# Filling a selective-scan pipeline: finer turns for TensorE and ScalarE, later sums from two banks

## The chip, the cores and the metric

One core of one Trainium2 chip. The metric is the device time of one launch in microseconds; lower is better.

## The reference

The input is four images of 64 x 64 positions with 128 channels, so 4 x 4096 tokens. The whole network is a Mamba-like layer, an attention layer and an expert layer with a residual sum after each. Only the first is touched by the change:

```python
x = x + _L0_conv_ref(_gn(x), ...)           # _gn: group norm, 32 groups

xz = einsum('pd,bld->bpl', in_proj_w, x)     # 256 channels x, 256 channels z
def mamba_dir(xz, ...):
    x, z = split(xz, 2)
    x = silu(causal_conv1d(x, conv_w, conv_b))           # 4 taps
    x_dbl = einsum('rd,bdl->brl', x_proj_w, x)           # 8 dt, 16 B, 16 C rows
    delta = softplus(einsum('dr,brl->bdl', dt_w, dt_raw) + dt_b)
    A = -exp(A_log)
    h = h * exp(delta * A) + (delta * x) * B             # scan over 4096 positions
    y = sum over 16 states of h * C
    return (y + D * x) * silu(z)
y = y_forward + y_backward + y_sliced        # three orders of the same tokens
out = einsum('od,bdl->blo', out_proj_w, y)
```

All is float32.

## The kernel before

The launch has four stretches. In the **fill**, the class Inputs makes what the scans of all four images need and writes it to DRAM, while the class Scans already runs the scans of image 0 beside it. In the **wide opening** the first attention input is made from image 0's sums. In the **main loop** attention of one image runs beside the scans of the next. An end part follows. The change lies in the fill and in the few lines around it.

**Inputs** handles an image in a norm (`norm`, L254 on), and then twelve chunks (three orders of four chunks with 1024 positions each, `of_chunk`). In a chunk, PE makes the convolution into two PSUM tiles `cv` (the input projection is folded into its taps), ACT makes `u` by Silu, PE makes the projection `xd` (copied by ACT to `xds`) and from it `dt`. The softplus is max(v, 0) + log(1 + exp(-|v|)), with a correction for the rounding of 1 + e: ACT makes `e` by Abs and then Exp, `r` by Relu, `ln` by Ln, and `s` in two Identity steps; PE adds e, -s and ln in PSUM (`sp`, L415), and DVE adds this to r (L417) and multiplies it with u (L421). Chunks of order 2 are each followed by a `gate`, which makes silu(z). These pieces are Python generators. `flow` (L79) keeps up to two of them active and takes one turn of each alternately; every yield ends a turn. A second piece may start when the youngest active one has had `apart` turns, in which turns that yield WAIT don't count, but plain waiting yields do. The PSUM tiles of Inputs are three tiles of two banks each that rotate; `held` counts those in use. `middle` lets only one chunk at a time be between dt and the last r.

**Scans** (`of_image`) runs 384 steps for an image: 3 orders x 4 chunks x 8 groups of channels x 4. A step handles 128 rows (16 channels x 8 states) of 1024 positions: ACT makes `dA` = exp(A delta) (L496, written in place into `delta` in odd steps), DVE multiplies `dB` = du x B (L505), scans to `h` (L508) and multiplies with C in place (L510). For each four steps PE sums over the states into a PSUM tile `y` (L516): the sums of steps 0 and 1 are issued at turn 1 of the next four steps, those of 2 and 3 at turn 2, and at the end of that turn DVE makes the output `o` (L532) and the bank goes back. `delta` has three buffers of two steps each, `du` four, `dB` three, dA two. For image 0 the loads of `du` are issued by ACT, all others by SP (L482).

Everything in the fill is issued in an order written out by hand, and each engine works its own queue in that order. Two `Pace` objects set it: per iteration 0.98 turns of the flow and one turn of the scans, a step of the scans being two turns:

```python
first = Pace(scans.of_image(0, inputs.made, nc.scalar))
others = Pace(flow(inputs.pieces(range(nb)), 2, 6))
while not first.done:
    others.run(0.98)
    first.run(1.0)
others.rest()
```

Of the kernel before, what the change touches and what calls it, by code (L numbers as in the profile page):

```python
# [81 lines left out]
WAIT = "wait"  # L82
# [52 lines left out]
def scan_weights(nc, const, load, load_ps, ident, in_proj_w, out_proj_w, dirs):  # L135

    w_z = const["fill"].tile([P, DI], F32, name="w_z")
    w_out = const["all"].tile([P, 2, C], F32, name="w_out")
    w_in = load.tile([P, 4, C], F32, tag="w_in", name="raw_in")
    nc.sync.dma_start(out=w_in, in_=in_proj_w.rearrange("(k p) c -> p k c", p=P))  # L140
    ps = load_ps.tile([P, 512], F32, tag="ps", name="ps_in")
    for m in range(2):
        nc.tensor.transpose(ps[:, m * P : (m + 1) * P], w_in[:, 2 + m, :], ident)
    nc.vector.tensor_copy(w_z, ps[:, :DI])
    raw = load.tile([P, DI], F32, tag="raw", name="raw_out")
    nc.sync.dma_start(out=raw, in_=out_proj_w)
    ps = load_ps.tile([P, 512], F32, tag="ps", name="ps_out")
    for m in range(2):
        nc.tensor.transpose(ps[:, m * P : (m + 1) * P], raw[:, m * P : (m + 1) * P], ident)
    nc.vector.tensor_copy(w_out.rearrange("p m c -> p (m c)"), ps[:, :DI])  # L150
    ws = []
    for i, d in enumerate(dirs):
        w = {}
        raw = load.tile([R + 2 * NS, DI], F32, tag="raw", name=f"raw_x{i}")
        nc.sync.dma_start(out=raw, in_=d["x_proj_w"])
        w["x"] = const["fill"].tile([P, 2, X_ROWS], F32, name=f"w_x{i}")
        nc.gpsimd.memset(w["x"], 0.0)
        for m in range(2):
            ps = load_ps.tile([P, 512], F32, tag="ps", name=f"ps_x{i}_{m}")
            k = R + 2 * NS  # L160
            nc.tensor.transpose(ps[:, :k], raw[:, m * P : (m + 1) * P], ident[:k, :k])
            for row, at, n in ((DT_ROW, 0, R), (B_ROW, R, NS), (C_ROW, R + NS, NS)):
                nc.vector.tensor_copy(w["x"][:, m, row : row + n], ps[:, at : at + n])
        raw = load.tile([P, 2, X_ROWS], F32, tag="raw_dt", name=f"raw_dt{i}")
        nc.gpsimd.memset(raw, 0.0)
        nc.sync.dma_start(out=raw[:, :, DT_ROW:], in_=d["dt_proj_w"].rearrange("(m p) r -> p m r", p=P))
        w["dt"] = const["fill"].tile([X_ROWS, 2, P], F32, name=f"w_dt{i}")
        ps = load_ps.tile([P, 512], F32, tag="ps", name=f"ps_dt{i}")
        for m in range(2):
            nc.tensor.transpose(ps[:X_ROWS, m * P : (m + 1) * P], raw[:, m, :], ident)  # L170
        nc.vector.tensor_copy(w["dt"][DT_ROW:].rearrange("r m p -> r (m p)"), ps[DT_ROW:X_ROWS, :DI])
        for name in ("conv_b", "dt_proj_b"):
            w[name] = const["fill"].tile([P, 2], F32, name=f"{name}{i}")
            nc.scalar.dma_start(out=w[name], in_=d[name].rearrange("(m p) -> p m", p=P))

        w["D"] = const["all"].tile([P, DI // 32], F32, name=f"D{i}")
        for g in range(4):
            nc.scalar.dma_start(out=w["D"][32 * g : 32 * g + 32], in_=d["D"].rearrange("(k p) -> p k", p=32))

        taps = load.tile([P, 2, 4], F32, tag="taps", name=f"taps{i}")  # L180
        nc.scalar.dma_start(out=taps, in_=d["conv_w"].rearrange("(m p) k -> p m k", p=P))
        w["conv"] = const["fill"].tile([P, 4, DI], F32, name=f"conv{i}")
        for k in range(4):
            ps = load_ps.tile([P, 512], F32, tag="ps", name=f"ps_cv{i}_{k}")
            for m in range(2):
                cut = load.tile([P, C], F32, tag="cut", name=f"cut{i}_{k}_{m}")
                nc.vector.tensor_scalar_mul(cut, w_in[:, m, :], taps[:, m, k : k + 1])
                nc.tensor.transpose(ps[:, m * P : (m + 1) * P], cut, ident)
            nc.vector.tensor_copy(w["conv"][:, k, :], ps[:, :DI])
        ws.append(w)  # L190
    for i, (d, w) in enumerate(zip(dirs, ws)):

        w["A"] = const["all"].tile([P, 2, NB // 2], F32, name=f"A{i}")
        a_log = d["A_log"].rearrange("(k d) (q n) -> d q n k", d=16, n=NS2)
        for c in range(16):
            for q, by in enumerate((nc.scalar, nc.gpsimd)):
                by.dma_start(out=w["A"][c * NS2 : (c + 1) * NS2, q, :], in_=a_log[c, q])
        nc.scalar.activation(w["A"], w["A"], AF.Exp)
        nc.vector.tensor_scalar_mul(w["A"], w["A"], -1.0)
    return w_z, w_out, ws  # L200


class Inputs:
# [28 lines left out]

    def bank(self, name):
        while self.held == 3:
            yield
        self.held += 1
        return self.ps.tile([P, T], F32, tag="a", name=name)

# [16 lines left out]
    def norm(self, b):  # L255

        nc = self.nc
        while b - 1 in self.gated and self.gated[b - 1] < NC:
            yield
        self.gated[b] = 0  # L260
        xin = self.x[b].rearrange("(t p) c -> p t c", p=P)
        xn = self.big.tile([P, L + 6], F32, tag="xn", name=f"xn_{b}")
# [51 lines left out]
    def gate(self, b, g):  # L314
        nc, xn = self.nc, self.normed[b]
        s_g = self.piece.tile([P, 2, T], F32, tag="u", bufs=2, name=f"z_{b}_{g}")
        for m in range(2):
            ps = yield from self.bank(f"z_{b}_{g}_{m}")
            for i in range(T // 512):
# [3 lines left out]
                    start=True, stop=True,  # L323
                )
            yield
            nc.scalar.activation(s_g[:, m, :], ps, AF.Silu)
            self.leave()
        nc.gpsimd.dma_start(out=self.sz[b].rearrange("(m p) t -> p m t", p=P)[:, :, g * T : (g + 1) * T], in_=s_g)
# [2 lines left out]

    def of_chunk(self, b, order, c):
        while b not in self.normed or (order == 2 and b not in self.sliced):
            yield
        src = self.sliced[b] if order == 2 else self.normed[b]
        nc, w, key = self.nc, self.ws[order], f"{b}_{order}_{c}"
        made = {
# [20 lines left out]
        for m in range(2):  # L358
            ps = yield from self.bank(f"cv_{key}_{m}")
            for g, cut in enumerate(halves):  # L360
                for k in range(4):
                    nc.tensor.matmul(  # L362
                        ps[:, cut], w["conv"][:, k, m * P : (m + 1) * P], reads(k, g), start=(k == 0), stop=(k == 3)
                    )
            banks.append(ps)
            yield
        for m in range(2):
            nc.scalar.activation(u[:, m, :], banks[m], AF.Silu, bias=w["conv_b"][:, m : m + 1])
            self.leave()
# [12 lines left out]
        yield  # L382

        while self.middle:
            yield
        self.middle = True

        e = self.piece.tile([P, 2, T], F32, tag="e", name=f"e_{key}")
# [14 lines left out]
        s = self.piece.tile([P, 2, T], F32, tag="s", name=f"s_{key}")  # L403
        ln = self.piece.tile([P, 2, T], F32, tag="ln", name=f"ln_{key}")
        nc.scalar.activation(e, e, AF.Exp, scale=-1.0)
        nc.scalar.activation(ln, e, AF.Ln, bias=1.0)
        yield
        nc.scalar.activation(s, e, AF.Identity, bias=1.0)
        nc.scalar.activation(s, s, AF.Identity, bias=self.minus_one)  # L409
        yield  # L410
        for m in range(2):
            ps = yield from self.bank(f"sp_{key}_{m}")
            for cut in halves:
                for i, (sign, t) in enumerate(((self.ident, e), (self.minus, s), (self.ident, ln))):
                    nc.tensor.matmul(ps[:, cut], sign, t[:, m, cut], start=(i == 0), stop=(i == 2))  # L415
            yield
            nc.vector.tensor_add(r[:, m, :], r[:, m, :], ps)  # L417
            self.leave()
        self.middle = False
        keep("delta", r)  # L420
# [6 lines left out]
class Scans:  # L427
# [20 lines left out]
            )  # L448
        self.sums, self.steps, self.did = {}, {}, set()

    def of_image(self, b, made, queue=None):

        nc = self.nc
        self.steps[b] = 0
# [15 lines left out]
        def load(s):  # L470
# [7 lines left out]
            for name, bufs in (("delta", 3), ("du", 4)):  # L478
                t = self.deep.tile([P, T], F32, tag=name, bufs=bufs, name=f"{name}_{b}_{s}")
                src = made[b, order, c][name][at : at + 16]  # L480
                by = queue if queue is not None and name == "du" else nc.sync
                by.dma_start(out=t, in_=src.unsqueeze(1).to_broadcast([16, NS2, T]))  # L482
                tiles[name, s] = tiles[name, s + 1] = t
            if j == 0:
# [71 lines left out]
        for s in range(self.AHEAD):  # L556
            yield from have(s)
            load(s)
        exp(0)
        y = None  # L560

        def sums(s):

            if s % 4 in (1, 2):
                first = s // 4 * 4 - 4 + (0 if s % 4 == 1 else 2)
                total(first, y)
                total(first + 1, y)

        for s in range(n):
            if s + self.AHEAD < n:  # L570
                yield from have(s + self.AHEAD)
            late = s >= 4 and s % 4 in (1, 2)
            if late and s % 4 == 1:
                while not self.bank.free:
                    self.did.add("wait")
                    yield
# [3 lines left out]
            if s + 1 < n:  # L580
                exp(s + 1)
                self.did.add("exp")
            if late:
                sums(s)
                self.did.add("sum")
            yield
            step(s)
            if late and s % 4 == 2:
                out(s - 3, y)
                self.bank.leave()  # L590
            yield
            self.steps[b] += 1
        while not self.bank.free:
            self.did.add("wait")
            yield
        y = self.bank.grab(f"y_{b}_{n}")
        for s in (n + 1, n + 2):
            sums(s)
            yield
        out(n - 1, y)  # L600
        self.bank.leave()
        self.steps[b] += 1


# [684 lines left out]
def tile_kernel(tc, ctx, x, in_proj_w, dirs, out_proj_w, attn, gate, weight1, weight2, out):  # L1289
# [8 lines left out]
    ident = const.tile([P, P], F32, name="ident")  # L1298
    make_identity(nc, ident)
    cols = column(nc, const, 1e-5, "eps"), column(nc, const, -0.5, "mhalf")  # L1300
    bank = Bank(ctx.enter_context(tc.tile_pool(name="bank", bufs=1, space=PSUM)), 1)
    all_const = ctx.enter_context(tc.tile_pool(name="w_all", bufs=1))
    ws = []
    scanning = ExitStack()
    scans = Scans(tc, scanning, ws, ident, bank, dram)
    with ExitStack() as fill:
        consts = {"all": all_const, "fill": fill.enter_context(tc.tile_pool(name="w_fill", bufs=1))}
        with tc.tile_pool(name="w_load", bufs=2) as load, tc.tile_pool(
# [2 lines left out]
            w_z, w_out, made = scan_weights(nc, consts, load, load_ps, ident, in_proj_w, out_proj_w, dirs)  # L1311
        ws.extend(made)
        inputs = Inputs(tc, fill, x, w_z, ws, cols, dram, ident)
        with tc.manual_schedule():
            first = Pace(scans.of_image(0, inputs.made, nc.scalar))
            others = Pace(flow(inputs.pieces(range(nb)), 2, 6))
            while not first.done:
                others.run(0.98)
                first.run(1.0)
            others.rest()  # L1320
    block = Attention(tc, ctx, attn, gate, cols, ident, bank, dram, t1, w_out, scans.sums, inputs.sz, x)

    following = Pace(*(scans.of_image(b, inputs.made) for b in range(1, nb)))
# [93 lines left out]
```

## Time and profile before

| | |
|---|---|
| median of 3 runs | 13271.63 us (13271.44 to 13279.25) |
| the profiled execution | 13276.74 us, of which span 13275.0 us |
| PE, DVE, ACT, POOL busy, share of the span | 93%, 68%, 81%, 26% |
| first scan of image 0 | at 148.94 us |
| last output of image 0's scans | at 2463.47 us |
| first activation of the main loop | at 2705.9 us |
| TensorE clock granted, whole span and fill | 0.947 and 0.86 |

The shares are means over stretches that differ. The fill, from 147.6 to 2463.9 us, is 17% of the span and the only stretch that the change touches beside the start. Lines "engine ... <- releaser" give idle time of an engine by what ended it: microseconds in total, times, longest.

### The profile page before, as it was taken

The numbers are of one execution on the slowest core, as the hardware profiler recorded it, in microseconds if no ns is written. First come the engines' busy times: TensorE is split into PE (matmuls) and PEld (weight loads), VectorE is DVE, ScalarE is ACT, GpSimd is POOL, SyncE is SP. The second block draws the span as 40 slices with busy tenths as digits, with TensorE's granted clock in tenths as the row PEclk, the third lists the DMA queues.
The fourth block names the chain that finished last, engine by engine and source line by source line (L and its number), as shares of the span: only waits on it lengthen the run. The fifth ranks groups of instructions, "written<-read, shape, count | busy, mean of one in ns | idle before, by whom it ended". The sixth has DMA issues, their size and how long they took to land. (4 is left out here: it accounts for less than half of the span.)

```text
span 13275.0 us, 213812 instructions
## 1 busy us (share of the span) xinstructions
PE 12311.7 (93%) x85255; PEld 3959.8 (30%) x85255; DVE 8963.1 (68%) x8565; ACT 10702.1 (81%) x10807; POOL 3471.0 (26%) x4198
## 2 busy tenths in 40 slices
PE   7797879489999999999999999999999999999976
PEld 3333333222222222233332222333222222222224
DVE  6998989788888876988888778888874110000014
ACT  5665756289999998999999989999998888888851
POOL 2333334222333332333333223333331000000001
PEclk9888888699999999999999999999999999999986
DMA  5666666544444445544444454444443100000015
GB/s 143 185 185 176 190 175 195 172 127 118 121 121 117 115 119 136 130 109 117 114 106 114 116 140 126 110 114 114 112 107 96 43 16 9 9 18 21 12 36 180
DMA packets 686881, 1482.04 MB, mean 112 GB/s; under 512 B 184894, under 2 KB 301942, under 8 KB 685878
## 3 DMA queue, kind: packets, MB, share of 16 engines
q1 hardware_dynamic: 495182, 1049.44, 30.7%
q0 software_dynamic: 139584, 300.84, 7.3%
q10 hardware_dynamic: 51112, 118.08, 3.3%
q8 instruction: 667, 10.93, 0.3%
q14 instruction: 336, 2.75, 0.1%
HBM read 1158.83 MB, written 308.94 MB: 111 GB/s over the span
## 5 line engine op out<-in xcount | busy, mean ns | idle before, releaser
L851 ACT ACTIVATE e<-s 128x1024 f32<-128x1024 f32 x8192 | 7904.5, 1027 | 1015.6 <-PE s L846 788.9
L846 PE MATMUL s<-qm,qT 32*128 32x512 f32 x32768 | 5416.4, 642 | 109.4 <-DMA qT<-d_q 58.8
L860 PE MATMUL acc<-e,v 128*32 128x512 f32 x32768 | 4387.0, 607 | 23.0 <-ACT av L869 20.0
L509 POOL COPY ends<-h 128x1 f32<-128x1 f32 x1536 | 1835.7, 1195 | 4934.0 <-DVE h L508 4920.3
L846 PEld LDWEIGHTS s<-qm,qT 32*128 32x128 f32 x32768 | 1789.8, 184 | 3266.4 <-issue 1453.6
L860 PEld LDWEIGHTS acc<-e,v 128*32 128x32 f32 x32768 | 647.6, 108 | 3158.2 <-issue 3019.3
L508 DVE TENSOR_TENSOR_SCAN h<-dA,ends,dB 128x1024 f32<-128x1024 f32 x576 | 1374.4, 2386 | 186.1 <-ACT dA L496 128.0
L508 DVE TENSOR_TENSOR_SCAN h<-delta,ends,du 128x1024 f32<-128x1024 f32 x576 | 1354.1, 2351 | 160.0 <-ACT delta L496 88.5
L505 DVE TENSOR_TENSOR dB<-du,B 128x1024 f32<-128x1024 f32 x768 | 935.3, 1218 | 204.3 <-PE y L516 185.8
L496 ACT ACTIVATE dA<-delta,A 128x1024 f32<-128x1024 f32 x768 | 887.9, 1156 | 213.5 <-DMA delta<-d_delta 152.2
L496 ACT ACTIVATE delta<-delta,A 128x1024 f32<-128x1024 f32 x768 | 887.3, 1155 | 180.7 <-PE y L516 170.2
L510 DVE TENSOR_TENSOR du<-h,C 128x1024 f32<-128x1024 f32 x768 | 940.7, 1225 | 26.3
L510 DVE TENSOR_TENSOR dB<-h,C 128x1024 f32<-128x1024 f32 x768 | 940.7, 1225 | 26.3
L505 DVE TENSOR_TENSOR du<-du,B 128x1024 f32<-128x1024 f32 x768 | 933.9, 1216 | 0.0
L875 POOL DMA_DIRECT2D d_ctx<-av x512 | 262.6, 521 | 1646.4 <-ACT av L869 1642.8
L362 PE MATMUL cv<-xn,conv 128*128 128x512 f32 x1024 | 492.2, 640 | 40.6 <-DVE xn L299 26.5
L516 PE MATMUL y<-dB,sel 128*32 128x256 f32 x6144 | 496.0, 396 | 16.4 <-DVE o L532 16.4
L516 PE MATMUL y<-du,sel 128*32 128x256 f32 x6144 | 492.0, 393 | 6.1 <-DVE du L510 6.1
L508 DVE TENSOR_TENSOR_SCAN h<-dA,dB 128x1024 f32<-128x1024 f32 x192 | 446.9, 2328 | 56.8 <-ACT dA L496 35.4
L532 DVE SCALAR_TENSOR_TENSOR o<-us,D,y 128x256 f32<-128x256 f32 x384 | 206.2, 537 | 412.1 <-PE y L516 398.6
L508 DVE TENSOR_TENSOR_SCAN h<-delta,du 128x1024 f32<-128x1024 f32 x192 | 440.1, 2292 | 38.9 <-ACT delta L496 15.3
L415 PE MATMUL sp<-s,minus 128*128 128x512 f32 x384 | 223.1, 665 | 208.2 <-ACT s L409 208.2
(248 smaller groups left out, 7714.6 us busy)
## 6 DMA issues: line engine op xcount, KB each, us to landing
delta<-d_delta SPq DMA_DIRECT2D x768, 512.0 KB
du<-d_du SPq DMA_DIRECT2D x576, 512.0 KB
du<-d_du ACTq DMA_DIRECT2D x192, 512.0 KB
d_u<-u POOLq DMA_DIRECT2D x48, 1024.0 KB, 5.7
B<-d_bc SPq DMA_DIRECT2D x96, 512.0 KB
C<-d_bc SPq DMA_DIRECT2D x96, 512.0 KB
d_delta<-r POOLq DMA_DIRECT2D x48, 1024.0 KB, 5.4
d_du<-u POOLq DMA_DIRECT2D x48, 1024.0 KB, 6.7
```

The costliest lines, as they stand in the source:

```text
L362: nc.tensor.matmul(ps[:, cut], w["conv"][:, k, m * P : (m + 1) * P], reads(k, g), start=(k == 0), stop=(k == 3))
L415: nc.tensor.matmul(ps[:, cut], sign, t[:, m, cut], start=(i == 0), stop=(i == 2))
L496: nc.scalar.activation(tiles["delta", s], t, AF.Exp, scale=A)
L505: nc.vector.tensor_mul(dB, du, spread[order, c, "B", j % 2])
L508: nc.vector.tensor_tensor_scan(h, dA, dB, first, ALU.mult, ALU.add)
L509: nc.gpsimd.tensor_copy(ends[order, c][:, at : at + 1], h[:, T - 1 :])
L510: nc.vector.tensor_mul(dB, h, spread[order, c, "C", j % 2])
L516: nc.tensor.matmul(y[32 * g : 32 * g + 32, : T // 4], self.sel[:, j // 2, :], hC[:, 256 * g : 256 * g + 256], start=(j == 0), stop=(j == 3),)
L846: nc.tensor.matmul(s_ps[:, k, :], qT[at : at + 32, kc * P : (kc + 1) * P], queries[j, qb][at : at + 32, :], start=True, stop=True,)
L851: nc.scalar.activation(e, s_ps, AF.Exp, scale=1.0 / math.sqrt(D))
L860: nc.tensor.matmul(accs[j, qb][32 * k : 32 * k + 32, :], v[:, kc, h * VW : h * VW + 32], es[i][k // 2][:, k % 2, :], start=(kc == 0), stop ...
L875: nc.gpsimd.dma_start(out=self.context[b][h * D : h * D + D, cut], in_=av[32 * k : 32 * k + D, :])
```

## The change

Five edits, all for the fill:

- Turns become smaller: a convolution and an sp group yield after each half of a tile (512 positions), with one more yield before ACT or DVE reads the tiles. Ln comes after s in a turn of its own. r is added for both halves of the channels after both sp groups. The gate has one more yield in each half.
- Yields that only wait become WAIT, which doesn't count for `apart`.
- `apart` goes from 6 to 10 and the pace from 0.98 to 1.5 turns per iteration.
- For image 0 (`alone`), the output o is made at turn 0 of the four steps after those in which the sums were issued, two steps later than before, with two banks for the sums. The fill gets a pool of its own for them; the single `bank` for later stretches is made after the fill.
- A's Exp and its negation move from `scan_weights` to the point in `of_image` just ahead of the first dA.

```diff
-        nc.scalar.activation(w["A"], w["A"], AF.Exp)
-        nc.vector.tensor_scalar_mul(w["A"], w["A"], -1.0)
     return w_z, w_out, ws
...
     def bank(self, name):
         while self.held == 3:
-            yield
+            yield WAIT
...
@@ gate
             yield
+            yield
             nc.scalar.activation(s_g[:, m, :], ps, AF.Silu)
@@ of_chunk
                     nc.tensor.matmul(
                         ps[:, cut], w["conv"][:, k, m * P : (m + 1) * P], reads(k, g), start=(k == 0), stop=(k == 3)
                     )
+                yield
             banks.append(ps)
-            yield
+        yield
         for m in range(2):
             nc.scalar.activation(u[:, m, :], banks[m], AF.Silu, bias=w["conv_b"][:, m : m + 1])
...
         nc.scalar.activation(e, e, AF.Exp, scale=-1.0)
-        nc.scalar.activation(ln, e, AF.Ln, bias=1.0)
         yield
         nc.scalar.activation(s, e, AF.Identity, bias=1.0)
         nc.scalar.activation(s, s, AF.Identity, bias=self.minus_one)
         yield
+        nc.scalar.activation(ln, e, AF.Ln, bias=1.0)
+        yield
+        banks = []
         for m in range(2):
             ps = yield from self.bank(f"sp_{key}_{m}")
             for cut in halves:
                 for i, (sign, t) in enumerate(((self.ident, e), (self.minus, s), (self.ident, ln))):
                     nc.tensor.matmul(ps[:, cut], sign, t[:, m, cut], start=(i == 0), stop=(i == 2))
-            yield
-            nc.vector.tensor_add(r[:, m, :], r[:, m, :], ps)
+                yield
+            banks.append(ps)
+        yield
+        for m in range(2):
+            nc.vector.tensor_add(r[:, m, :], r[:, m, :], banks[m])
             self.leave()
@@ of_image
+        if b == 0:
+            for w in self.ws:
+                nc.scalar.activation(w["A"], w["A"], AF.Exp)
+                nc.vector.tensor_scalar_mul(w["A"], w["A"], -1.0)
         exp(0)
...
+        def finish(s, y):
+            out(s, y)
+            self.bank.leave()
...
-            late = s >= 4 and s % 4 in (1, 2)
-            if late and s % 4 == 1:
+            turn = s % 4 if s >= 4 else None
+            if turn == 1:
...
             step(s)
-            if late and s % 4 == 2:
-                out(s - 3, y)
-                self.bank.leave()
+            if turn == 2 and not alone:
+                finish(s - 3, y)
+            if turn == 0 and alone and s >= 8:
+                finish(s - 5, y)
             yield
             self.steps[b] += 1
+        if alone:
+            finish(n - 5, y)
@@ tile_kernel
-    bank = Bank(ctx.enter_context(tc.tile_pool(name="bank", bufs=1, space=PSUM)), 1)
...
+        scans.bank = Bank(fill.enter_context(tc.tile_pool(name="s_bank", bufs=2, space=PSUM)), 2)
         with tc.manual_schedule():
-            first = Pace(scans.of_image(0, inputs.made, nc.scalar))
-            others = Pace(flow(inputs.pieces(range(nb)), 2, 6))
+            first = Pace(scans.of_image(0, inputs.made, True))
+            others = Pace(flow(inputs.pieces(range(nb)), 2, 10))
             while not first.done:
-                others.run(0.98)
+                others.run(1.5)
                 first.run(1.0)
             others.rest()
+    bank = scans.bank = Bank(ctx.enter_context(tc.tile_pool(name="bank", bufs=1, space=PSUM)), 1)
```

## The prediction

> **What bounds the kernel now.** I read the busy time of the engines by stretches, then the waits of VectorE (DVE) in the scan stretch, then the timelines of the places where it stands still. The stretches: start, fill with the scans of image 0, wide opening, main loop.
>
> ```profile
> 0.00:147.60 147.60, 89.23 (x212) 40.90 (x212) 29.08 (x90) 31.26 (x28) 37.26 (x75) 0.90 0.34 79
> 147.60:2463.90 2316.30, 1921.87 (x6641) 774.27 (x6641) 2118.35 (x1457) 1480.85 (x1190) 810.35 (x942) 0.86 0.64 184
> 2463.90:2705.90 242.00, 39.31 (x200) 30.90 (x202) 162.81 (x327) 22.90 (x18) 45.96 (x59) 0.54 0.57 161
> 2705.90:12813.00 10107.10, 9993.55 (x76612) 2941.63 (x76610) 6444.02 (x6164) 9115.55 (x9493) 2508.55 (x3004) 0.99 0.36 92
> ...
> 1360.00:1560.00 200.00, 196.30 (x638) 79.81 (x637) 193.57 (x131) 146.44 (x116) 77.58 (x97) 0.93 0.68 201
> ```
>
> The third and following numbers are PE, PEld, DVE, ACT, POOL busy. The change touches only the first two stretches, and what follows needs image 0's sums, so time saved before 2463.9 shifts all the rest. In the last line, a good stretch, DVE is busy 96.8%, which is as full as it gets (the rest is gaps of some 0.1 us between instructions). Over the whole fill it is 91.5%. So DVE sets the pace; the waits say what is missing:
>
> ```profile
> DVE o L532 <- PE y L516: 57.9, 22, 5.1
> DVE r L417 <- PE sp L415: 31.9, 14, 6.6
> DVE h L508 <- ACT dA L496: 22.3, 8, 3.9
> DVE dB L505 <- DMA du<-d_du: 18.3, 1, 18.3
> DVE h L508 <- ACT delta L496: 12.9, 12, 3.9
> DVE dB L505 <- PE y L516: 8.0, 3, 2.8
> ```
>
> Without the 18.3, which is the first load ahead of scan 0, and with four small rows that add 3, DVE waits **136 us** in the fill. That is all that the change can win there: 2316 - 136 = 2180, and 2118/2180 is 97%, the fullness of the good stretch. The waits sit in a few places. At an image's beginning (672 to 745) there are five:
>
> ```profile
> 688.88 0.48 DVE L532 SCALAR_TENSOR_TENSOR o<-us,D,y 128x256 f32<-128x256 f32 x1 [4.87 <-PE y L516]
> ...
> 706.82 1.23 DVE L505 TENSOR_TENSOR dB<-du,B 128x1024 f32<-128x1024 f32 x1 [2.82 <-PE y L516]
> 709.78 2.35 DVE L508 TENSOR_TENSOR_SCAN h<-dA,ends,dB 128x1024 f32<-128x1024 f32 x1 [1.73 <-ACT dA L496]
> ...
> 717.61 0.48 DVE L532 SCALAR_TENSOR_TENSOR o<-us,D,y 128x256 f32<-128x256 f32 x1 [4.22 <-PE y L516]
> ```
>
> and on TensorE (PE) their cause:
>
> ```profile
> 672.26 15.55 PE L362 MATMUL cv<-xn,conv 128*128 128x512 f32 x32 [8.13 <-DVE xn L299]
> ...
> 688.74 14.01 PE L362 MATMUL cv<-xn,conv 128*128 128x512 f32 x32
> ```
>
> Two chunks' convolutions go back to back, because the second chunk's waiting turns count towards its distance (6), so both start in lockstep. The same happens at the start: 29.37 us of convolution for two chunks before one projection.
>
> **What the Trainium skill says.** "TensorE: Matmul & The Clock Gate", part 1, says that an idle PE falls to half clock after about 3.4 us and takes about as long to warm up. The trace agrees: after an 8.38 us wait a pair of sp matmuls took 2.07 us, warm 1.02. The same page (architectural detail) calls ACT and DVE strict FIFOs; the trace agrees: a u that waited 13.76 us for cv held the dA behind it. "ScalarE: Activation LUTs", "What ACT_TABLE_LOAD costs", gives 1.28 us plus a drain of 1.38; here loads take 1.283 and no drain shows (u's load ran at 692.62 right after an ACTIVATE that ended at 692.61), so I use 1.28. "PSUM — Partial Sum Buffer" (specifications) gives 8 banks of 2 KiB: three double tiles and two sum banks just fit; no trace of before shows all 8 in use.
>
> **The change part by part.** An iteration is one turn of the scan, half a scan step, about 2.44 us of DVE. I wrote the turns of both versions out from the code, as an order without times; durations below are the rows' (cv half 3.44, xd or dt 3.44, sp half 2.58, y 1.0, Exp or Ln 1.91, s 1.9 and 2.0, dA 1.15 us).
>
> 1. *Pace and groups.* A chunk has 12 turns before at 0.98 per iteration (12.2 iterations), 19 after at 1.5 (12.7); a chunk with its gate 15 and 24 (15.3 and 16). Scan 0 comes at iteration 41 before, 29 after. The fill work ends at iteration 802 of 811 before, 793 of 799 after, so neither leaves a tail and no scan lacks its chunk. The same matmuls, activations, DMAs and DVE work are issued; table switches go from about 250 to 243: nothing.
>
> 2. *WAIT not counted, distance 10.* The first chunk no longer shares its path with the second. Before, from the convolution's start at 57.7 to u's end at 129.4: 71.7 us. After: convolution 15.7 (73.4, as the trace has it for two tiles), Silu 1.1, xd 3.4, its copy 1.2, dt 1.9 until the first abs, abs/relu 4.1, Exp with its load 3.2, s twice 3.9, Ln with load 3.2: ln ready at 95.7 - 1 (point 4) = 94.7. Then PE: ln pair 0.9, cv 3.4, sp 2.6, sp 2.6, xd of the next chunk 3.4, sp 2.6: 110.3. Then r 1.2 and u 2.3: 113.9. **Gain 15.5 us** including point 4's one. The load path of 18.3 us behind it stays.
>  At the three later images the chain from xn to the chunk's last r before was cv of two chunks 29.6, y 2, xd twice and dt 10.3, ACT 17, sp 10.3: 69 us, against 22 iterations of DVE, 11 steps of 4.88 and two o: 55. That is 14 short, and the trace shows 16.4 of waits from 672 to 745. After: cv and y 16.5, u 1.1, xd and its copy 4.4, dt 1.7, ACT 15, ln pair 0.9, cv 3.4, sp 2.6, y 1, sp 2.6, xd 3.4, sp 2.6: 55, against xn 2.4, ten steps and two o: 52. The 3 missing and dA waits behind the Exp group overlap, an estimate of 6 together; about 1.8 more come in, as the norm's small DVE steps now follow each other with only PE or POOL between (0.8 and 1.0 in the start's trace). I leave **8 per image, 24 in all**.
>
> 3. *Sums later, two banks.* o comes two steps (9.7 us) later than before; its longest wait is 5.1. The next reader of the same deadline is dB, whose three buffers make it wait for the turn-1 sums one step back, as before. Those waits are 8.0 in all. So most of 57.9 goes, apart from what is left in point 2. In the tail one o more, 0.5 us.
>
> 4. *A's Exp and negation moved.* ACT no longer waits in its queue for A's loads (about 1 us ahead of the xn copies at 46.95; the 48 loads that it issues itself stay, so not the whole 16 us shown there). At their new place three Exps of 0.23 and three DVE products of 0.2 stand ahead of the first dA. Behind them only dA waits, which then ends near 141; du lands at 147.6 minus the gain, 7 us later. Cover: that load.
>
> 5. *Ln after s, and r for both halves at the end.* The PE queue waits for ACT 216 us at sp before; with y behind it. By my sum of work between dt and sp that falls from 7.0 to 6.1 us a chunk: no gain taken. The r wait: counted from dt to the last r, before had 25.9 to 31.2 us of DVE work for a chain of 31 to 36; after has 31 to 41 for 30 to 46, a mean shortfall of 1.6 against 4.4. So **most of 31.9 goes**. The price: three rotating tiles mean that the next chunk's dt takes the tile that r frees. Before, r was 3 or 5 iterations ahead of that dt; now 0 or 1. So PE starts each chunk level with DVE. For a usual chunk, from r's end: dt 1.9, two cv 6.9, y 1.0, cv 3.4, two sp pairs 1.7, ln pair 0.9 (ln itself is ready at 14.9 by ACT's sum), cv 3.4, y 1.0, two sp 5.2, xd 3.4, sp 2.6: 31.6. DVE until r: u 2.25, seven steps of 4.88, two o 0.94, first r 1.2: 38.5. Slack 7; a cold PE takes 1.5 to 3 of it. The tightest, the last chunk of order 1, has some 3. I take no stall here, but 16 us in all for chunks that fall short and for the first chunk after scan 0 (about 4). Bounds: 0, and 6 us for each of 30 such handovers, 180.
>
> Left over: 24 + 16 + 5 for gates = 45 of 136, so 91 gained; with 15.5, **107 us**. The profiled execution is 13276.7, 5 us above the median of 13271.6; I take the gain off the median: **13165**.
>
> **The rivals.**
> - *The waits move* (chance 0.10): o no longer waits, but PE is as late as before and dB, one step later, pays. Its unchanged deadline speaks for it, its 8.0 us against. Only the start is won: 13271.6 - 15.5 = 13256, no change by the bound below.
> - *Half* (0.22): cold PE and dA waits keep 91 of the 136: 13271.6 - 45 - 15.5 = 13211.
> - *The handover r to dt decides* (0.06): in each of 30 handovers the chain runs past its budget. It needs 44.5 us for 31.6, as with PE at half clock through most of the chain. Then 30 x 6 = 180 lost, against at most 136 - 29 + 15.5 = 122 won: 58 slower, **13329**. It decides from 122/30 = 4.1 us per handover. For it: PE's clock is 0.86 in the fill; against: 7 us of slack, and only 3.7 us of PE waits for r at dt before.
> - *All of it* (0.10): 136 + 15.5 less 10: 13130.
>
> **How the numbers follow.** The main case has 0.52. About 0.2% (26.5 us) is what a measurement of this kernel tells from no change. Faster: main, half, all: 0.84 and some of the first rival, 0.86. Same 0.07, slower 0.07. The range leaves out the slow case and half of each end: 13122 to 13250.
>
> **What would show it.** In the profile after: the first scan near 132 instead of 148.9; the end of image 0's scans near 2357; o's wait for y under 10 us, r's for sp under 20; no 64 convolution matmuls in a row at an image's beginning; PE waiting for r at dt some 30 times. Wrong: r's wait for sp above 60 us with a count near 30 (the handover), or dB's wait for y above 40 (moved waits).

## The result, and the profile after

The changed kernel takes **13169.17 us** (median of 4 runs, 13162.28 to 13172.54) against 13273.36 us before (4 runs, 13271.44 to 13279.25): ratio 0.992, 95% interval 0.9903 to 0.9937. That is 104 us, or 0.8%; the forecast was 13165 us and a gain of 107. The profiled execution after took 13172.54 us with a span of 13170.8, before 13276.74 with 13275.0: 104 us by either.

The fill and the 240 us behind it, by stretches as before (PE, PEld, DVE, ACT, POOL busy):

```profile
132.00:2360.00 2228.00, 1940.31 (x6627) 771.50 (x6625) 2110.32 (x1448) 1463.71 (x1174) 812.72 (x937) 0.87 0.66 191
2360.00:2600.00 240.00, 38.81 (x200) 30.15 (x200) 166.88 (x333) 25.97 (x22) 49.77 (x64) 0.54 0.56 155
```

DVE does 2110 us of work in 2228 us, where before it did 2118 in 2316: 94.7% busy instead of 91.5%. What it still waits for between its first scan and its last output:

```profile
DVE h L513 <- ACT dA L501: 16.5, 12, 3.3
DVE h L513 <- ACT delta L501: 14.1, 8, 3.3
DVE r L422 <- PE sp L417: 9.1, 6, 2.8
...
DVE dB L510 <- PE y L521: 6.4, 5, 2.4
DVE gms L291 <- PE gv L289: 3.1, 3, 1.6
DVE gms L283 <- PE gm L281: 2.2, 3, 0.7
...
DVE o L537 <- PE y L521: 0.6, 1, 0.6
```

With three small rows that is 55 us, against 136. o's wait has gone from 57.9 to 0.6, r's from 31.9 to 9.1; h's, now the largest, from 35.2 to 30.6. The start, on DVE:

```profile
103.18 1.22 DVE L422 TENSOR_TENSOR r<-r,sp 128x1024 f32<-128x1024 f32 x1 [43.99 <-PE sp L417]
111.77 1.22 DVE L422 TENSOR_TENSOR r<-r,sp 128x1024 f32<-128x1024 f32 x1 [7.36 <-PE sp L417]
113.02 2.29 DVE L426 TENSOR_TENSOR u<-r,u 128x2048 f32<-128x2048 f32 x1
...
133.21 1.23 DVE L510 TENSOR_TENSOR dB<-du,B 128x1024 f32<-128x1024 f32 x1 [8.25 <-DMA du<-d_du]
134.54 2.29 DVE L513 TENSOR_TENSOR_SCAN h<-dA,dB 128x1024 f32<-128x1024 f32 x1
```

The first u ends at 115.3 (before: 129.4) and the first scan starts at 134.5 instead of 148.9. On PE two rows tell the most (waits in the fill):

```profile
PE dt L394 <- DVE r L422: 55.3, 19, 5.5
PE sp L417 <- ACT ln L410: 44.9, 17, 3.1
```

The first is the hand-over of a tile from r to the next dt, 3.7 us before the change. The second with its siblings (s 25.8, e 8.2, u and z 5.5) makes 84 us in which PE stands at sp for ACT; before it was 216:

```profile
PE sp L415 <- ACT s L409: 203.2, 26, 10.6
...
PE sp L415 <- ACT e L405: 13.0, 7, 3.6
```

PE also no longer makes two chunks' convolutions in one run at the start: 32 convolution matmuls stand in a row at 57.17, where there were 64.

So of the 104 us, 14.4 come from the start and 81 from DVE's waits. The last output of image 0 ends at 2365.2 instead of 2464.1, so 98.9 are there at the end of the fill. DVE is also busy for 3.7 us less from the first scan to that output (2113.7 instead of 2117.3), which makes up the 3.5 us between. The other 5 or so appear later and lie within what executions of one kernel differ by.

### The profile page after: what moved, and what is told of

It is laid out like the page before. It is cut to its first block, busy times and chain, and to the rows that moved or that the text cites. A ratio compares the mean times of both kernels' runs of the same rounds, so it can differ in the third digit from the quotient of the medians.

```text
span 13170.8 us, 213908 instructions
## 1 busy us (share of the span) xinstructions
PE 12323.5 (94%) x85255; PEld 3949.4 (30%) x85255; DVE 8961.4 (68%) x8565; ACT 10693.2 (81%) x10800; POOL 3474.2 (26%) x4198
## 5 line engine op out<-in xcount | busy, mean ns | idle before, releaser
L996 DVE TENSOR_SCALAR h<-h,b 128x512 f32<-128x512 f32 x96 | 71.8, 748 | 497.0 <-PE s L861 496.8
```

## The experiments

A name with b_ is the kernel before with some of the parts put in; one with a_ is the changed kernel with a part undone or a further step. DVE's waits below are counted, as above, from the first scan to image 0's last output. "Before" took 13277 to 13280 us beside these runs, so times are compared by their ratio to it. The interval of a ratio is 0.0006 to 0.0017 to either side, 8 to 23 us. Taken together (root of the sum of squares), those of the changed kernel and of a kernel a_ come to about 0.0023, 30 us: a smaller difference between them is not resolved, and what is said of it rests on the waits of one profiled execution each.

| kernel | median us | ratio to before (95%) | DVE waits us | of them o, r, dB, h for PE or ACT |
|---|---|---|---|---|
| before | 13273.4 | 1 | 136 | 58, 32, 8, 35 |
| b_wait | 13270.7 | 0.9993 (0.9985 to 1.0002) | 146 | 29, 66, 16, 30 |
| b_late | 13269.7 | 0.9994 (0.9986 to 1.0003) | 138 | 0, 53, 24, 60 |
| b_both | 13261.7 | 0.9987 (0.998 to 0.9993) | 141 | 1, 80, 19, 39 |
| b_rlate | 13242.8 | 0.9971 (0.996 to 0.9982) | 121 | 0, 4, 35, 80 |
| changed | 13169.2 | 0.992 (0.9903 to 0.9937) | 55 | 1, 9, 6, 31 |
| a_early | 13172.5 | 0.9921 (0.9907 to 0.9936) | 57 | 20, 4, 4, 23 |
| a_ln | 13185.3 | 0.993 (0.9915 to 0.9944) | 76 | 0, 3, 1, 65 |
| a_groups | 13194.7 | 0.9936 (0.9919 to 0.9953) | 73 | 1, 1, 28, 37 |
| a_halves | 13206.5 | 0.9948 (0.9931 to 0.9964) | 90 | 0, 57, 2, 23 |
| a_gate | 13227.8 | 0.9961 (0.9947 to 0.9975) | 109 | 0, 44, 13, 41 |
| a_six | 13213.0 | 0.9949 (0.9935 to 0.9964) | 91 | 0, 24, 29, 22 |
| a_dt | 13194.8 | 0.994 (0.9925 to 0.9955) | 81 | 0, 24, 17, 22 |
| a_act | 13197.8 | 0.9938 (0.9921 to 0.9954) | 76 | 0, 16, 18, 35 |

**One part alone: WAIT (b_wait).**

```diff
 # bank, norm, of_chunk (twice), in the kernel before
-            yield
+            yield WAIT
```

> The kernel before with one edit: the four waiting yields become WAIT (distance 6 and pace 0.98 stay). My theory (each edit cures its own waits): the lockstep at the beginnings goes, so the first scan comes 10 to 15 us earlier (134 to 139 instead of 148.9) and the waits at the three image beginnings fall by some 15 us together, while o's wait for y elsewhere and r's for sp stay: DVE's waits in the fill 110 to 125 of 136, time 20 to 40 us below before. Rival 'fine turns do it': only the start moves, 10 to 15 us, waits 130 or more.

Measured: the first scan comes at 134.84 us, all 14 us of the start, but the fill ends at 2460.6, only 3.5 earlier. DVE's waits:

```profile
DVE r L417 <- PE sp L415: 66.0, 23, 7.8
DVE o L532 <- PE y L516: 29.2, 13, 5.3
...
DVE dB L505 <- PE y L516: 15.5, 4, 6.5
```

o's wait halves as the lockstep goes, and r's doubles. My theory gave 20 to 40 us and was wrong. That with turns as large as before the chunks, no longer in lockstep, meet at other places would fit; no run shows it.

**One part alone: late sums from two banks (b_late).**

```diff
-            if late and s % 4 == 2:
+            if late and s % 4 == 2 and not alone:
                 out(s - 3, y)
                 self.bank.leave()
+            if alone and s % 4 == 0 and s >= 8:
+                out(s - 5, y)
+                self.bank.leave()
...
```

> The kernel before with one edit: two banks for the sums in the fill and o two steps later. My theory: o's wait for y (57.9 us) goes nearly to zero, but dB, h and r keep theirs and dB takes a small part; DVE's waits 136 to about 85, 45 to 55 us below before, first scan unchanged at 148.9. Rival 'the waits move': o's wait goes, dB's wait for y rises from 8 to 40 or more, and the time stays within 15 us of before. Rival 'fine turns do it': as 'the waits move'.

```profile
DVE r L417 <- PE sp L415: 53.1, 35, 7.1
DVE h L508 <- ACT dA L496: 32.8, 15, 3.9
DVE h L508 <- ACT delta L496: 27.1, 14, 3.6
DVE dB L505 <- PE y L516: 23.6, 9, 6.4
```

o no longer waits at all, and the sum of the waits is 138 instead of 136. The rival "the waits move" holds for this part, though dB takes only 16 of them; r takes 21 and h 25. The row of 57.9 us was where DVE met a late PE first, not what made PE late.

**Undone: late sums (a_early).**

```diff
-            if turn == 2 and not alone:
+            if turn == 2:
                 finish(s - 3, y)
-            if turn == 0 and alone and s >= 8:
-                finish(s - 5, y)
...
-        if alone:
-            finish(n - 5, y)
```

> The changed kernel with one part undone: o again at the end of turn 2, right after its sums (two banks stay). My theory: o's wait for y returns in part, 20 to 40 us, since the lockstep is gone but PE is still level with DVE at each hand-over: time 15 to 35 us above the changed kernel. Rival 'fine turns do it': below 10 us more. Rival 'late sums do it': 50 us or more.

```profile
DVE o L537 <- PE y L521: 19.6, 11, 3.1
```

o waits 19.6 us again and r, dB and h 15 less, so DVE's waits are 57 and the time is the changed kernel's within the interval. My theory (15 to 35 us slower) was wrong; below 10 is what 'fine turns do it' said. o's late place, half of the change's name, is worth next to nothing in it. The second bank stays in this run, so it is not tested alone.

**Undone: r after both groups (a_halves).**

```diff
-            banks.append(ps)
-        yield
-        for m in range(2):
-            nc.vector.tensor_add(r[:, m, :], r[:, m, :], banks[m])
-            self.leave()
+            nc.vector.tensor_add(r[:, m, :], r[:, m, :], ps)
+            self.leave()
...
-                others.run(1.5)
+                others.run(1.41)
```

> The changed kernel with r added for each half as soon as its own sp group is issued (no shared point after both), so that the first sp tile is free some five iterations before the next dt; pace 1.41 instead of 1.5, so that the work ends at the same iteration (793 of 799 counted). If the hand-over from r to dt costs what I left for it (some 16 us of waits), PE's wait for r at dt (55 us after) falls below 25 and the time by 0 to 15 us. If the hand-over is free, the time stays within 5 us. If adding r early brings back r's wait for sp (before: 31.9 us), the time rises by 10 to 25 us.

```profile
DVE r L418 <- PE sp L416: 57.2, 19, 9.0
DVE h L509 <- ACT delta L497: 12.9, 6, 3.5
```

PE's wait for r at dt falls to 3.0 us, as the first reading says, but r's wait for sp is back with 57 us, and the kernel is 0.3% slower than the changed one by their ratios. The third reading holds in kind, with more than its 10 to 25 us: 37 by the ratios. The pace is lower here as well, and the first scan comes 4.5 us earlier, at 130.0. What the hand-over costs by itself this run cannot say, since r's wait came back with the cure.

**Undone: Ln's place (a_ln).**

```diff
         nc.scalar.activation(e, e, AF.Exp, scale=-1.0)
+        nc.scalar.activation(ln, e, AF.Ln, bias=1.0)
         yield
...
         yield
-        nc.scalar.activation(ln, e, AF.Ln, bias=1.0)
         yield
```

> The changed kernel with Ln back beside Exp, ahead of s, and an empty turn where Ln stood, so that all other turns stay. PE's wait for ACT at sp fell from 216 us (before) to 77 us (after). Theory 'order of Ln': it makes that fall; then the wait returns to 130 us or more and the time rises by 25 to 60 us. Theory 'place of r' or 'size of groups': the wait stays under 110 us and the time within 10 us of the changed kernel.

PE's wait for ACT at sp is 113 us, against 84 after (the 77 in the expectation is too low) and 216 before: between the two readings. DVE's waits rise by 20 us; h alone waits 34 more, r and dB together 12.5 less:

```profile
DVE h L513 <- ACT dA L501: 34.9, 8, 7.3
DVE h L513 <- ACT delta L501: 29.1, 10, 8.0
```

The longest single wait goes from 3.3 to 8.0 us. Ahead of the dA for which h waits 7.3 us, Exp, a table load, Ln and a load back stand in one group from 677.69 to 684.12. The time is 16 us above the changed kernel's, under what the intervals resolve.

**Undone: the size of PE's groups (a_groups).**

```diff
                         ps[:, cut], w["conv"][:, k, m * P : (m + 1) * P], reads(k, g), start=(k == 0), stop=(k == 3)
                     )
-                yield
+            yield
+            yield
             banks.append(ps)
...
-                yield
+            yield
+            yield
             banks.append(ps)
```

> The changed kernel with both halves of a convolution tile and of an sp tile issued in one turn, followed by two yields, so that the number of turns, the pace and the places of ACT's and DVE's work stay and only PE's groups are twice as large. Theory 'size of groups': 40 to 80 us slower than the changed kernel, o, r and dB waiting for PE as before. Theory 'place of r' (the turns give each reader more time): within 15 us.

```profile
DVE dB L512 <- PE y L523: 27.6, 9, 6.7
```

dB waits 21 us more. At its longest wait the sums y are issued at 1865.0, behind a whole sp tile of 5.2 us (2.6 for the half of one in the changed kernel) and, ahead of that, 15.5 us of convolution. The time is 25 us up by the medians, 21 by the ratios, between the two theories, but less than those 30 us; so it is the 18 us more of DVE's waits that say that the size counts, and r and o wait no more than in the changed kernel.

**Together, and with r late, on large turns (b_both, b_rlate).** b_both is b_wait and b_late in one; b_rlate adds r's later place:

```diff
+        banks = []
...
             yield
-            nc.vector.tensor_add(r[:, m, :], r[:, m, :], ps)
+            banks.append(ps)
+        yield
+        for m in range(2):
+            nc.vector.tensor_add(r[:, m, :], r[:, m, :], banks[m])
             self.leave()
...
-                others.run(0.98)
+                others.run(1.05)
```

> The kernel before with WAIT and with late sums from two banks, turns as large as before, pace 0.98, distance 6. Alone each moved its waits to other rows and won 8 and 9 us. Theory 'turns' (size or place): together they win 10 to 25 us, r's wait for sp stays at 50 us or more. Theory 'they need each other': 50 us or more won.

> b_both with r for both halves added after both sp groups and one more turn, pace 1.05 for the additional turn (the work ends at iteration 798 of 806 counted). Theory 'place of r': r's wait for sp falls below 20 us and the time to 60 to 100 us below before. Theory 'size of groups': r's wait falls but dB, o or h take it over, less than 35 us below before. If the hand-over from r to dt is what I priced, PE's wait for r at dt appears here with 40 us or more.

b_both wins about what the start gives, 0.13%, and DVE still waits 141 us, 80 of them at r, as the theory 'turns' said:

```profile
DVE r L417 <- PE sp L415: 79.9, 40, 7.7
```

In b_rlate r's wait falls to 3.5, but

```profile
DVE h L512 <- ACT delta L500: 45.9, 17, 6.0
DVE dB L509 <- PE y L520: 34.5, 15, 6.8
DVE h L512 <- ACT dA L500: 33.9, 15, 4.0
```

take most of it over: 121 us in all, 0.16% better than b_both. The gain lies between the two theories' numbers, and the waits move as "size of groups" says. PE's wait for r at dt is 13.5 us here, not the 40 expected.

**The hand-over and finer ACT groups, tried on the changed kernel (a_dt, a_act).**

```diff
 # a_dt
         self.middle = True
+        yield
...
-                others.run(1.5)
+                others.run(1.54)
 # a_act: abs and relu of each half in its own turn, s in two turns
-        yield
+            yield
...
         nc.scalar.activation(s, e, AF.Identity, bias=1.0)
+        yield
...
-            others = Pace(flow(inputs.pieces(range(nb)), 2, 10))
+            others = Pace(flow(inputs.pieces(range(nb)), 2, 12))
...
-                others.run(1.5)
+                others.run(1.62)
```

> The changed kernel with one more turn between the wait for middle and dt, pace 1.54 for it (the work ends at iteration 791 of 798 counted, 793 of 799 without): dt is issued 1 to 2 iterations after the r that frees its tile instead of 0 to 1. PE's wait for r at dt (55 us) falls below 30 in any case. If the hand-over costs time, it is 5 to 15 us faster than the changed kernel; if it is covered, as the price of nothing says, within 5 us; if a shorter way from dt to r costs more than the hand-over, r's or h's wait rises and it is 5 us or more slower.

> The changed kernel with smaller ACT groups as well: abs and relu of each half in a turn of its own, the two s steps in two turns; pace 1.62 and distance 12 for the two additional turns (ends at iteration 791 of 798 counted). What is left of DVE's waits is mostly h for ACT (30.6 of 55.1 us), dA standing behind ACT's groups. Theory 'size and order of ACT's groups': h's wait falls to 10 to 20 us and the time by 8 to 20 us. Theory 'ACT itself waits for PE there': h's wait stays over 25 us and the time within 6 us.

In a_dt PE's wait for r falls only to 41.0 us, not below 30 as was expected in any case. DVE's waits rise from 55 to 81, 15 of them at r: of the readings the last. But more than the hand-over has changed:

```profile
PE sp L418 <- ACT ln L411: 84.4, 17, 6.9
```

The additional turn and the faster pace have also moved the gate's first Silu directly ahead of Ln (z at 542.85 and Ln at 545.18, for one), at 12 of the 47 Ln in the trace; in the changed kernel it stands there nowhere. PE's wait for Ln goes from 44.9 to 84.4 us with it. So the run doesn't tell what the hand-over costs, and a_gate below meets the same order. In a_act h waits 35 us and not 10 to 20; r and dB take 18 more. The ratios of both are 0.2% above the changed kernel's, which is not resolved; their waits are 26 and 21 us longer. So smaller turns are not better by themselves.

**The gate's yield and the distance (a_gate, a_six).** Size, Ln and r's place don't account for all that separates b_rlate (121) from the changed kernel (55).

```diff
 # a_gate
             yield
-            yield
             nc.scalar.activation(s_g[:, m, :], ps, AF.Silu)
 # a_six
-            others = Pace(flow(inputs.pieces(range(nb)), 2, 10))
+            others = Pace(flow(inputs.pieces(range(nb)), 2, 6))
...
-                others.run(1.5)
+                others.run(1.54)
```

> The changed kernel without the additional yield in each half of the gate (pace stays 1.5; the work ends at iteration 788 of 799 counted, 793 with it). From the coarse kernel with r placed late (121 us of DVE's waits) to the changed kernel (55) are 66 us; the size of PE's groups and Ln's place, each undone alone, account for 18 and 20. If the gate's yield holds part of the remaining 28: 8 to 25 us slower, by h's or dB's waits in the last third of each image. If the rest is only that these parts don't add up: within 6 us.

> The changed kernel with the distance between two chunks back at 6 turns, pace 1.54 so that no work is left at the end (ends at iteration 795 of 802 counted). With 19 turns in a chunk, 6 puts two chunks closer together, so that their convolutions and sp groups meet. If the distance holds part of the remaining 28 us: 10 to 40 us slower, first scan 5 to 10 us later (139 to 145 us instead of 134.5). If not: within 6 us.

a_gate loses most of all edits, 0.4%: 54 us by the ratios, twice the most that was expected, and in r's waits more than in h's or dB's. Its trace on ACT in image 0's third order shows one way:

```profile
551.08 1.28 ACT L324 ACT_TABLE_LOAD   x1
552.37 1.02 ACT L324 ACTIVATE z<-z 128x1024 f32<-128x1024 f32 x1
553.40 1.28 ACT L409 ACT_TABLE_LOAD   x1
554.70 1.91 ACT L409 ACTIVATE ln<-e 128x2048 f32<-128x2048 f32 x1
```

The gate's first Silu now comes ahead of Ln, with a load of its own, so Ln ends 2.3 us later than it would. This is so at 10 of the 47 Ln in the trace. In the changed kernel Ln is ready first and z follows:

```profile
546.55 1.91 ACT L410 ACTIVATE ln<-e 128x2048 f32<-128x2048 f32 x1
...
548.48 1.28 ACT L325 ACT_TABLE_LOAD   x1
549.77 1.02 ACT L325 ACTIVATE z<-z 128x1024 f32<-128x1024 f32 x1
```

PE, in its turn, waits longer for Ln (91.6 us against 44.9), and DVE's r for PE (43.8 against 9.1); the waits of PE, then of DVE, in a_gate:

```profile
PE sp L416 <- ACT ln L409: 91.6, 17, 6.9
```

```profile
DVE r L421 <- PE sp L416: 43.8, 17, 5.9
```

In the stretches in which the chunks of order 2 are made (430 to 660 us, 1010 to 1240, 1590 to 1820) DVE waits 19, 19 and 17 us, against 6, 8 and 7. The yield also gives an order-2 chunk 24 turns instead of 22, and so more of the scans' time. No run parts these two, but a_dt says that the order is not all: it keeps the yield and has Silu ahead of Ln as often, PE waits for Ln nearly as long, and DVE's waits rise by 26 us, not 54.

```profile
DVE dB L510 <- PE y L521: 29.3, 12, 5.4
DVE r L422 <- PE sp L417: 24.0, 7, 5.4
```

These are a_six's rows. It loses 0.3%, 38 us by the ratios, within the 10 to 40 expected for a distance that matters; that two chunks' PE work meets again fits the rows. Its first scan comes at 138.2, a little earlier than expected.

## Why the prediction was right, and where it was not

**The sum.** 107 us forecast, 104 measured. The start: 15.5 forecast, 14.4 measured; the chain of point 2 holds link by link (last r forecast to begin when sp ends at 110.3, measured 111.77). The waits: 91 forecast to go, 81 gone; 45 forecast to stay, 55 stayed. The image beginnings keep 6 to 8 us each in dA, dB and r and 1.5 to 2.6 in the norm's small steps, against the 8 that I had left for each.

**The split was wrong.** The total came out because I had bounded it by the sum of DVE's waits, not because each edit cured its row; that it came within 3 us is in part luck. Point 3 said that o's late place removes "most of 57.9". In the changed kernel that row is gone, but a_early shows that its place is worth 2 us of DVE's waits, and b_late that alone it is worth nothing: 57.9 went and 60 came elsewhere. The first rival, "the waits move", which I gave a chance of 0.10, describes this part of the change in b_late, except that it named dB alone as the next one to pay.

**Point 2** left 24 us of waits at the image beginnings and took the rest as gained by WAIT and the distance. The lockstep does go, but b_wait shows that WAIT alone lowers no sum of waits (146 us), and on large turns most of the waits stay with late sums (b_both, 141 us) and with r late as well (b_rlate, 121). On small turns the distance is worth 36 us of waits (a_six). No run has the distance of 10 on large turns, or the changed kernel without WAIT.

**Point 5 failed twice.** It took no gain from PE's wait at sp, by a sum that fell from 7.0 to 6.1 us a chunk; measured it fell from 4.5 to 1.8 (216 and 84 us over 48 chunks). My sum counted work and not when ACT comes to it; how much of the fall is Ln's place is seen in a_ln, 29 of 132 us. r's place, to which it gave "most of 31.9", is the largest single part within of_chunk: 35 us. The price there was right in kind: PE waits for r at dt 55 us in 19 places (some 30 forecast). What DVE pays for it stays open. In all it waits for PE at r, dB and o for 16 us (9.1, 6.4 and 0.6), which is just what I had left for the hand-over, and neither a_halves nor a_dt tells how much of that it is. The rival that ends slower had its mechanism, but not its size: 16 us are far from its 180, so the chain fits, as its 7 us of slack said.

**The gate** was left 5 us of waits, and its yield was counted on for nothing. Undone alone it is worth 54 us of DVE's waits, the most of any part. That step I had not priced at all; I counted its turns (15 and 24) and not what they put ahead of Ln.

**Point 4** was hidden as said: the moved Exps ran at 122.96, dA was done at 124.6, and du landed at 133.2. The gain ahead of the xn copies is 0.5 us, not 1: they start at 46.49 instead of 46.95, since a table load of 1.28 us that A's Exp had drawn now stands directly ahead of them.

The parts, each undone alone from the changed kernel, cost DVE 2 (sums), 18 (groups), 20 (Ln), 35 (r), 36 (distance) and 54 us (gate): 165 where only 81 were won. They don't add up, so undoing one part also spoils what the others give. The pace moved along with r and the distance, so that the work ends at the same place, and was not tried alone. Why exactly this spacing is good was not settled: the two further steps that the runs tried (finer ACT turns, a later dt) each make DVE wait longer, and none of the kernels run beats the changed one.

## What to carry to other kernels

In a pipeline whose engines each work a fixed order, read the sum of all waits of the engine that sets the pace as the room to win, and not its rows as a list of cures: a row tells where that engine first meets a late partner, and a later reader can just move the wait to the next row, as in b_late. Look for what makes the partner late, here PE standing at sp for ACT and long groups of matmuls in front of the short sums, and give a consumer its turn only when the producer's whole group can be done. Before pricing an inserted turn at nothing, write out what it puts ahead of what in each queue.

## What the runs showed of the hardware

With A's Exp moved away, the first plain copy on ACT has a table load of its own directly ahead of it (1.28 us at 45.20). In the kernel before, the trace has no load between the one for the Exp at 24.62 and the copies at 46.95, so that one served the copies too. Moving the Exp away did not save a load at the start, it put one closer to the path.
